# Softmax reciprocals turned on their way through DRAM, unscaled queries, and a later load, in an attention kernel on one core

## Chip, core and metric

The kernel runs on one NeuronCore of a Trainium2 chip; the other seven are idle. The metric is the device time of one launch in microseconds (us). Before the change it is 2303.48 us, the median of three runs (2294.57, 2303.48, 2305.79).

## The reference

One block of a transformer, all in float32, with x of 2048 rows by 256 columns, 16 heads of width 128, and a feed-forward part of width 704. Cut to what is computed:

```python
xn = (x - mean(x)) / sqrt(var(x) + 1e-5)
qkv = xn @ Wqkv.T                          # q, k, v: 2048 x 16 x 128 each
logits = q @ k.T * 128 ** -0.5             # each head: 2048 x 2048
w = softmax(logits)
att = (w @ v) @ Wout.T                     # 2048 x 256
Q(w) = clip(round(w / (mean(|w|) + 1e-8)), -1, 1)
ffn = (sigmoid(xn @ Q(w1).T) * (xn @ Q(w2).T)) @ Q(w3).T
out = x + att + ffn
```

## The kernel before

**Stages.** A lead-in of some 100 us normalizes x, turns it (the tile `xnT`, features on partitions), makes q, k and v of the first heads and does the feed-forward part, whose result waits in DRAM. Then come 64 *blocks*: 16 heads, in each four blocks of 512 queries. A block has four *steps* of 128 queries; `n` numbers blocks, `t` the steps of a block, `h` heads, `b` the block in its head, `v` the steps. Scores run six steps (`LEAD`) ahead of the weighting by v, so one pass of the main loop works on two blocks at once.

**A step of scores** (`scores`): TensorE multiplies the step's 128 queries by all 2048 keys, into two PSUM tiles `s` of 128 x 1024. DVE takes the maximum of each (L630, into the two columns of `mx`) and then the negated larger one (L633, `nm`); ACT takes the exponential with `nm` as bias and the row sums as a second output (L640, into `p`). Sixteen DMAs, ten from SP's queue and six from ACT's (`exchanged`, L659), move the pieces of `p` into `part`, with partitions exchanged, and DVE transposes 32 x 32 blocks of `part` into `R` (L706).

**Weighting.** Products are made by a scheme of the Strassen kind: seven products of half size in place of eight. It needs sums and differences of the operands. POOL makes those of `R` (`differences`, L726: T1, T2, T3 and T4, some in halves), of v once a head (`v_combined`, L748) and of weights and of `xnT` (`weight_sums`, `sums_of`, `x_sums`). TensorE multiplies (`weighted`, L773) into the PSUM tile `av`; ACT copies one half of partial results to SBUF (`copied`, L791, into `oU`) and DVE adds the other (`added`, L799). After the fourth step DVE multiplies by the reciprocals of the row sums (L801), and the block's result is sent to DRAM (`put_away`, L827, tile `od`). It comes back later for the output projection.

**The reciprocals.** `inverses(n)` sums the two halves of the row sums on DVE (L673), takes the reciprocals (L674, four columns of a 32-column tile `ri`), transposes 32 x 32 blocks (L676, into `riT`), and sends four rows from each group of 32 partitions to DRAM with four DMAs from POOL's queue (L678, tile `rd` of 4 x 128). `spread(n)` brings the 512 numbers of a block back to all 128 partitions (L685, into `oT`). The multiply L801 then makes `oT` from `oU` and `oT`.

**Queries and keys of later heads** are made by the same kind of scheme during the steps of the head before. `fast_product` makes one product at a time in a PSUM bank (`ps_m`, one buffer), and `fast_read` adds it on DVE to what stands in `kTs` and `qTs` (L200, L197). Queries carry the factor SCALE = 128 ** -0.5, keys do not; so where a query sum starts from a key sum, `fast_scaled` (L223) copies it with the factor, once for two blocks of a head, 28 times in all.

**Order.** The order on each engine is the order of the code (`manual_schedule`). What a step leaves to do (`left`: `added`, the second read, `fast_scaled`) is done at the head of the next step, ahead of its scores. POOL's order in a block is: at step 0 `put_away` of the block before, T1b, T3b, parts of `v_combined`, and the first half of T2; at step 1 the rest of T2, T4, then `spread`; at step 2 the four DMAs of `inverses` of the next block; at step 3 T1a and T3a of the next block. Between these stand DMAs and sums for other stages (`between`). All of these DMAs are issued by POOL, in order.

**The last head** has no later head's products; its projection is done at once. `fetched_back(b)` brings the feed-forward part and the other heads' sum back (L924, into `xnT`) and x for the final sum (L925, into `sofar`), at step 2 of the block before; `opened(b, ...)` uses both at steps 0 and 3 of the block after (L944: DVE adds to `sofar`). Its last four blocks are multiplied by the reciprocals in `projected` (L964), not at L801.

## Time and profile before

One profiled execution: 2299.23 us by its own time, of which the span from the first to the last instruction is 2297.5 us; the granted TensorE clock was 0.992 of full speed.

| Engine | busy, us | share of the span |
|---|---|---|
| TensorE (PE) | 2189.6 | 95% |
| VectorE (DVE) | 1887.3 | 82% |
| GpSimd (POOL) | 1765.6 | 77% |
| TensorE weight loads (PEld) | 1094.3 | 48% |
| ScalarE (ACT) | 744.9 | 32% |

| Stretch of the span, us | PE busy | DVE busy | POOL busy |
|---|---|---|---|
| 0 to 170 (lead-in, first scores) | 162.07 | 109.90 | 44.28 |
| 170 to 2180 (blocks) | 1920.44 | 1708.12 | 1660.55 |
| 2180 to 2297.5 (last head) | 107.03 | 69.25 | 60.80 |

How to read it: a group is a line of the code, an engine, an operation and `out<-in` by the names of tiles, with the number of instructions, the busy time, the mean duration of one in ns, and the idle time of the engine just before them with what ended it. A wait `X <- Y` says that X's engine stood idle until Y ended. PEld are TensorE's weight loads, which run ahead of the matmuls; PEq, DVEq and so on are the engines' instruction queues; "issue" is time in which nothing that the profile shows was waited for. Matmuls overlap each other, so a busy PE is not PE at its peak. The issue of a DMA by POOL counts as POOL work.

### The profile page before, as it was taken

The numbers are of one execution on the slowest core, as the hardware profiler recorded it, in microseconds if no ns is written. First come the engines' busy times: TensorE is split into PE (matmuls) and PEld (weight loads), VectorE is DVE, ScalarE is ACT, GpSimd is POOL, SyncE is SP. The second block draws the span as 40 slices with busy tenths as digits, with TensorE's granted clock in tenths as the row PEclk, the third lists the DMA queues.
The fourth block names the chain that finished last, engine by engine and source line by source line (L and its number), as shares of the span: only waits on it lengthen the run. The fifth ranks groups of instructions, "written<-read, shape, count | busy, mean of one in ns | idle before, by whom it ended". The sixth has DMA issues, their size and how long they took to land.

```text
span 2297.5 us, 41411 instructions
## 1 busy us (share of the span) xinstructions
PE 2189.6 (95%) x13514; PEld 1094.3 (48%) x13514; DVE 1887.3 (82%) x2562; ACT 744.9 (32%) x1390; POOL 1765.6 (77%) x1376
## 2 busy tenths in 40 slices
PE   9999999999999999899998999999999999999898
PEld 6744444454445444455444544444444544445455
DVE  6577888888788888789888888888888788888764
ACT  5543332333232323323333233332333233323331
POOL 0167878887788887988788887888789788898773
PEclk9999999999999999999999999999999999999999
DMA  2166667676676767776677766767677676776764
GB/s 89 55 151 155 150 179 196 166 208 158 175 205 173 189 161 190 193 193 184 162 184 187 199 175 174 198 173 191 159 183 210 171 185 161 189 194 184 193 172 123
DMA packets 246568, 398.46 MB, mean 173 GB/s; under 512 B 80720, under 2 KB 85264, under 8 KB 246352
## 3 DMA queue, kind: packets, MB, share of 16 engines
q1 hardware_dynamic: 127664, 174.95, 29.9%
q0 software_dynamic: 43792, 118.93, 18.6%
q10 hardware_dynamic: 74896, 101.94, 17.3%
q8 instruction: 106, 1.74, 0.3%
q14 instruction: 110, 0.90, 0.1%
HBM read 77.66 MB, written 49.41 MB: 55 GB/s over the span
## 4 chain that ended last, share of the span: by engine, by line
PE 28%; POOL 23%; DMA 19%; DVE 14%; issue 7%; SPq 5%; ACT 2%; ACTq 2%; DVEq 0%; POOLq 0%
DMA part<-p 17%; POOL R L726 14%; PE s L94 10%; PE av L773 8%; SPq L659 5%; DVE mx L630 4%; DVE R L706 3%; POOL st L748 2%; PE ph L508 2%; ACTq L659 2%; ACT p L640 2%; PE pow L94 1%; DVE oU L799 1%; PE pvw L94 1%; PE pw L94 1%
## 5 line engine op out<-in xcount | busy, mean ns | idle before, releaser
L726 POOL TENSOR_TENSOR R<-R 128x1024 f32<-128x1024 f32 x441 | 1181.6, 2686 | 37.0 <-DVE R L706 17.1
L640 ACT ACTIVATE p<-s,nm 128x1024 f32<-128x1024 f32 x512 | 566.2, 1111 | 1381.8 <-DMA part<-p 924.0
L94 PE MATMUL s<-kT,qT 128*64 128x512 f32 x4000 | 946.2, 594 | 13.9 <-ACT p L640 13.7
L630 DVE TENSOR_REDUCE mx<-s 128x1 f32<-128x1024 f32 x512 | 613.1, 1218 | 182.3 <-PE s L94 168.1
L706 DVE STREAM_TRANSPOSE R<-part 128x1024 f32<-128x1024 f32 x512 | 605.2, 1220 | 48.4 <-DMA part<-p 44.9
L94 PEld LDWEIGHTS s<-kT,qT 128*64 128x64 f32 x4000 | 331.1, 137 | 529.0 <-issue 442.1
L773 PE MATMUL av<-R,st 128*64 128x256 f32 x3024 | 495.9, 388 | 53.7 <-POOL R L726 50.2
L773 PE MATMUL av<-R,v 128*64 128x256 f32 x3728 | 539.7, 379 | 0.4 <-DVE oU L799 0.3
L773 PEld LDWEIGHTS av<-R,v 128*64 128x64 f32 x3728 | 341.9, 137 | 186.5 <-issue 56.7
L773 PEld LDWEIGHTS av<-R,st 128*64 128x64 f32 x3024 | 297.7, 139 | 208.1 <-POOL R L726 77.4
L678 POOL DMA_DIRECT2D rd<-r x240 | 124.8, 527 | 162.4 <-DVE r L676 162.1
L827 POOL DMA_DIRECT2D od<-oT x60 | 34.5, 575 | 157.7 <-DVE oT L801 150.2
L799 DVE TENSOR_TENSOR oU<-av,oU 64x256 f32<-64x256 f32 x248 | 101.1, 408 | 54.5 <-ACT oU L791 51.9
L911 DVE TENSOR_TENSOR osums<-pow,osums 128x512 f32<-128x512 f32 x196 | 124.6, 677 | 0.6 <-PE pow L94 0.6
L791 ACT COPY oU<-av 64x256 f32<-64x256 f32 x248 | 91.0, 367 | 94.4 <-PE av L773 90.1
L94 PE MATMUL pw<-t,ws 128*64 128x512 f32 x336 | 109.2, 592 | 0.0
L640 ACT ACTIVATION_READ_ACCUMULATOR p<-s,nm 128x1 f32 x512 | 100.2, 196 | 0.0
L160 POOL TENSOR_TENSOR t<-xnT 128x512 f32<-128x512 f32 x4 | 5.1, 1270 | 107.2 <-DMA part<-p 107.2
L315 DVE TENSOR_TENSOR v<-pvw,v 128x512 f32<-128x512 f32 x98 | 65.1, 676 | 24.9 <-PE pvw L94 24.9
L94 PE MATMUL pw<-xnT,wk 128*64 128x512 f32 x224 | 67.5, 599 | 14.2 <-DVE kT L200 14.2
L200 DVE TENSOR_TENSOR kT<-pw,kT 128x512 f32<-128x512 f32 x112 | 76.9, 686 | 1.8
L842 POOL TENSOR_TENSOR o<-o 128x512 f32<-128x512 f32 x56 | 71.7, 1280 | 0.5
(165 smaller groups left out, 1630.8 us busy)
## 6 DMA issues: line engine op xcount, KB each, us to landing
part<-p SPq DMA_DIRECT2D x2556, 64.0 KB, 2.2
part<-p ACTq DMA_DIRECT2D x1540, 64.0 KB, 2.5
oT<-rd POOLq DMA_DIRECT2D x60, 256.0 KB, 4.3
od<-oT POOLq DMA_DIRECT2D x60, 256.0 KB, 3.6
o<-od POOLq DMA_DIRECT2D x60, 256.0 KB, 4.4
vd<-v POOLq DMA_DIRECT2D x112, 128.0 KB, 3.6
xnT<-vd POOLq DMA_DIRECT2D x56, 256.0 KB, 5.2
osums<-yd POOLq DMA_DIRECT2D x28, 512.0 KB, 6.2
```

The costliest lines, as they stand in the source:

```text
L94: nc.tensor.matmul(out[c * HP : (c + 1) * HP], lhs[:, c * HP : (c + 1) * HP], rhs, start=start, stop=stop, skip_group_check=True,)
L200: nc.vector.tensor_tensor(k, pk, base, ALU.add)
L630: nc.vector.tensor_reduce(mx[:, i : i + 1], s, AX.X, ALU.max)
L640: nc.scalar.activation(p, s, AF.Exp, bias=nm, accum_out=sums[n][:, t, i : i + 1],)
L659: queue.dma_start(parts[v][g // 2][bass.ts(j, 32), g % 2, :], ps[j // 2][bass.ts(g, 32), bass.ts(j % 2, S // NQ)],)
L678: nc.gpsimd.dma_start(rds[n % 2][:, bass.ts(j, 32)], riT[32 * j : 32 * j + TB, :])
L706: nc.vector.transpose(to[:, t % 2, 2 * i : 2 * i + 2], part.rearrange("p g (s c) -> p g s c", s=2),)
L726: nc.gpsimd.tensor_tensor(o, x, y, ALU.subtract)
L773: nc.tensor.matmul(av[i * HP : (i + 1) * HP, half], l[:, kk], moving(s, kk), start=start, stop=(k == units[r] - 1), skip_group_check=True,)
L791: nc.scalar.copy(u[op, oq], av[ap, half])
L799: nc.vector.tensor_tensor(u[p, q], av[p, half], u[p, q], ALU.add)
L911: nc.vector.tensor_tensor(y, pm, y, ALU.add)
```

## The change

It does four things. (1) `rd` becomes 128 x 32 and `inverses` sends all of `riT` there with one DMA; `spread` reads, for each group of 32 partitions, the first four rows (128 numbers), and puts the four runs side by side in `oT`, so that `oT` now lies in the order (group, step, query in the group); the multiply reads it through a view in turned order. (2) The multiply writes to `oU` in place, and `put_away` sends `oU`; `oT` holds only reciprocals. (3) Queries are kept without SCALE: copies and plain additions stand where scaling ones stood, `fast_scaled` is gone (the first sum of `q1` reads `k1` directly), the exponential has `scale=SCALE`, and `nm` is made by one two-step scalar operation: the larger of the two columns of `mx` times -SCALE. (4) In the last head the load of x is moved from step 2 to step 3.

```diff
@@ q_piece
-        nc.scalar.activation(qT, pm, AF.Copy, scale=SCALE)
+        nc.scalar.copy(qT, pm)
@@ fast_read
         def q_sum(q, base):
-            nc.vector.scalar_tensor_tensor(q, pm, SCALE, base, ALU.mult, ALU.add)
+            nc.vector.tensor_tensor(q, pm, base, ALU.add)
...
         elif (b % 2, i) == (0, 1):
             if not second:
-                q_sum(q1, q0)
+                nc.vector.tensor_tensor(
+                    q1.rearrange("p (k j r) -> p k j r", j=P // 32, r=32), pk, k1, ALU.add
+                )
             else:
                 q_sum(q0, q1)
...
-    def fast_scaled(h: int, b: int):
-        c = b // 2 * 2
-        k1 = kTs[h].rearrange("p (j k r) -> p k j r", j=P // 32, r=32)[:, (c + 1) * TB : (c + 2) * TB]
-        q0 = qTs[h, c].rearrange("p (k j r) -> p k j r", j=P // 32, r=32)
-        nc.vector.tensor_scalar(q0, k1, SCALE, None, ALU.mult)
@@ tiles in DRAM
-    rds = [away.tile([TB, P], F32, tag=f"rd{i}", name=f"rd{i}") for i in range(2)]
+    rds = [away.tile([P, 32], F32, tag=f"rd{i}", name=f"rd{i}") for i in range(2)]
@@ scores
-        nc.vector.tensor_reduce(nm, mx, AX.X, ALU.max, negate=True)
+        nc.vector.tensor_scalar(nm, mx[:, 0:1], mx[:, 1:2], -SCALE, ALU.max, ALU.mult)
...
-                p, s, AF.Exp, bias=nm, accum_out=sums[n][:, t, i : i + 1],
+                p, s, AF.Exp, bias=nm, scale=SCALE, accum_out=sums[n][:, t, i : i + 1],
@@ inverses, spread
         nc.vector.transpose(riT, ri)
-        for j in range(P // 32):
-            nc.gpsimd.dma_start(
-                rds[n % 2][:, bass.ts(j, 32)], riT[32 * j : 32 * j + TB, :]
-            )
+        nc.gpsimd.dma_start(rds[n % 2], riT)
...
-            nc.gpsimd.dma_start(oT, rds[n % 2].rearrange("t p -> (t p)").partition_broadcast(P))
+            r = rds[n % 2].rearrange("(j c) r -> j (c r)", c=32)[:, : TB * 32]
+            nc.gpsimd.dma_start(
+                oT.rearrange("p (j x) -> p j x", j=P // 32), r.partition_broadcast(P)
+            )
@@ added
         if r == 3 and n < NBK - NB:
-            nc.vector.tensor_tensor(oT, u, rbs[n], ALU.mult)
+            u = u.rearrange("p (t j r) -> p t j r", t=TB, r=32)
+            r = rbs[n].rearrange("p (j t r) -> p t j r", t=TB, r=32)
+            nc.vector.tensor_tensor(u, u, r, ALU.mult)
@@ put_away
-        nc.gpsimd.dma_start(ods[h % (2 * G)][b], oT)
+        nc.gpsimd.dma_start(ods[h % (2 * G)][b], oU)
@@ fetched_back, between
         nc.gpsimd.dma_start(xnT[:, :, bass.ts(b, QB)], yds[b])
+
+    def x_fetched(b: int):
         nc.gpsimd.dma_start(
             sofar[b], x[b * QB : (b + 1) * QB, :].rearrange("(t p) d -> p t d", p=P)
         )
...
         if t == 2 and last - 1 <= n < last + NB - 1:
             fetched_back(n + 1 - last)
+        if t == 3 and last - 1 <= n < last + NB - 1:
+            x_fetched(n + 1 - last)
@@ the main loop, in left
-                if seven and product is fast_product and (b % 2, v % TB) == (0, 0):
-                    fast_scaled(h + 1, b)
```

## The prediction

> **What bounds the kernel now.** I read the page first, then the sums of waits, then the chain of waits stretch by stretch. From the page, the engines' busy shares and the chain that ended last:

> ```profile
> PE 2189.6 (95%) x13514; PEld 1094.3 (48%) x13514; DVE 1887.3 (82%) x2562; ACT 744.9 (32%) x1390; POOL 1765.6 (77%) x1376
> PE 28%; POOL 23%; DMA 19%; DVE 14%; issue 7%; SPq 5%; ACT 2%; ACTq 2%; DVEq 0%; POOLq 0%
> ```

> TensorE is busy 95% of 2297.5 us, so 107.9 us of it is idle, lead-in and tail included. What an edit on DVE or POOL can give is that idle time, and only where that engine ends it. The sums of waits say which engine does:

> ```profile
> PEld s L94 <- issue: 442.1, 1563, 0.6
> ...
> PEld av L773 <- POOL R L726: 77.4, 60, 4.6
> ...
> PEld s L94 <- ACT p L640: 40.9, 52, 7.0
> ...
> PEld pw L94 <- DVE kT L200: 27.3, 15, 4.0
> ...
> PEld pw L94 <- DVE qT L197: 13.9, 27, 1.0
> ...
> PEld pvw L94 <- DVE qT L197: 7.7, 14, 0.7
> ```

> (Columns: total us, times, longest.) An ordinary gap between two weight loads is 442.1/1563 = 0.28 us, with no one waited for; only what a wait has beyond it stops TensorE. The change takes work from POOL (L678) and DVE (L223); their costliest rows:

> ```profile
> L678 POOL DMA_DIRECT2D rd<-r x240 | 124.8, 527 | 162.4 <-DVE r L676 162.1
> L223 DVE TENSOR_SCALAR qT<-kT x28: 427/1596/1660, 230.3 to 2065.4; 128x512 f32<-128x512 f32 x28
> ```

> The first (from the page) issues four DMAs a block, 4 x 0.52 = 2.08 us, mostly after POOL has waited about 3 us for L676. The second (the answer on that line; min/median/max ns) is bimodal: 427 ns once, with POOL idle, and 1286 to 1660 ns in the 27 others, each of which began inside a POOL subtraction and ended about 0.3 us after it. At 1045.57 it took 1.60 us while POOL's subtraction begun at 1044.50 still had 1.31 us to run. So L223 waits for POOL.

> **The change, part by part.** The sum is made against the profiled execution: 2299.2 us, span 2297.5 us; that is 4.3 us under the median 2303.5 of the three runs.

> *One transfer of reciprocals (L678).* Three of four issues go. The one that stays covers 128 partitions, like L827 (575 ns mean), so 2.08 - 0.58 = 1.50 us a block, 90 us of POOL in 60 blocks. That counts only where POOL runs without a wait from there until TensorE waits for it. In most blocks the next thing POOL meets is the issue of od, which waits for the multiply (L827 waits 150.2 us in 44 blocks): the saving becomes a longer wait there. It passes where the weight sums and V's combinations fill that wait; the chain shows such a stretch:

> ```profile
> 1075.73 2.05 POOL rd L678 x4
> ...
> 1094.45 1.23 POOL st L748
> 1095.67 4.65 POOL R L726 x2
> 1100.33 0.04 issue
> 1100.37 1.72 PE av L773 x13
> ```

> Between the first and the last of these lines stand only POOL's pieces and short issue times, 25 us of them, and TensorE waits at its end (1.7 us of PE idle in 1094 to 1102). It recurs seven times (near 281, 552, 827, 1098, 1369, 1641, 1914), with 1.7 to 2.2 us of PE idle each: 7 x 1.5 = 10.5 us gained. In the sister stretch near 940 to 968 POOL waits for a landing (xnT<-vd) behind the same issues, so nothing is gained there. The landing of rd matters nowhere: it is read some 26 us later. Bounds: 0 and 77.4, all of the waits for POOL.

> *The spread.* It reads four 512-byte rows where it read 2 KB, so four times the pieces for each partition. Its issue takes 566 ns now; the costliest POOL issue in the trace is L925 at 777 ns, so 0 to 0.2 us a block, 12 us of POOL. It is covered by POOL's 3 us wait for L676 right behind it; without that cover, 7 x 0.2 = 1.4 us. I take 0. The landing (4.3 us) has about 17 us before the multiply.

> *L223 gone.* 28 x 1.463 = 41.0 us off DVE, at the head of a step, ahead of both maxima, nm and the read of the next product (L197), whose bank TensorE needs. Those are the two qT lines above: (13.9 - 27 x 0.28) + (7.7 - 14 x 0.28) = 6.3 + 3.8 = 10 us. What is late next is TensorE itself, whose loads then follow at 0.28 us. Bounds: 0, and 41 if all of L223 were on the path. L197 becomes a plain addition: 684 ns to the 677 to 686 ns of L911 and L200, nothing; the first addition reads k1 where it read q0, the same.

> *nm (L633).* A reduction of two elements, 155 ns, 256 times, becomes a two-step scalar operation with one operand read per partition. One element through such an operation with constants took 153 ns:

> ```profile
> L462 DVE TENSOR_SCALAR neg<-pos x3: 153/153/154, 27.1 to 34.9; 128x1 f32<-128x1 f32 x3
> ```

> An operand per partition adds about 55 ns: an element costs 1.045 ns (L801, 692 ns for 512, against L412, 161 for 4); L475 with such an operand takes 1819 ns for 1536 elements, so 214 beyond its elements, and L411 without one 163 for 4, so 159. That makes 208 ns, +53 ns a step, 14 us of DVE. It meets TensorE where a wait ends on DVE's reads (kT 15, v 8, osums 8 times) or on exponentials that waited for nm (72 of the 242 long waits there, hence some 16 of 52): 47 x 0.053 = 2.5, say 3 us. Bounds: 0 and 14, if it never waits for POOL; that is the rival below. I take the no-wait row because the fixed part of the operations that ran at two elements a cycle is larger: 427 - 267 = 160 ns (L223), and 163 and 162 (L465: 954 ns for 1408 elements, 1020 for 1536, less 55 for the operand). L462 has 153 - 1 = 152: it looks like the ordinary mode, and DVE's one-input work in that mode did not wait for POOL: L676 takes 211 to 213 ns in all 60 blocks.

> [...] No row of this trace shows a one-element operation beside POOL.

> *Result kept in oU, sent from oU.* The multiply keeps its size (L801: 693 ns median, up to 1693 where POOL runs beside it). But ACT's first copy of the next block (L791) now waits until od has been read. Matching rows: od is issued 0.99 us after the multiply starts, lands 3.6 us later (2.7 to 6.0), and the copy starts at about 6.3 us: 1.8 us to spare at the median. In 11 of 60 blocks the landing would be late, 8.1 us together, 2.0 at most. Behind the copy on ACT stand six exchange DMAs and the next exponentials; TensorE needs it only after the next 3.4 us of scores. I take 2 us; bounds 0 and 8.1.

> *x a step later.* Three of the four loads now queue on POOL behind T1a and T3a. From 2160.2, 2196.0, 2235.0 and 2268.4 they move to about 2170, 2204.9, 2240.6 and 2268.4. With landings of 8.5 us (5.6 to 12.2), and the additions (L944) at 2180.2, 2212.5, 2245.3 and 2279.0, DVE waits about 0, 0.9, 3.8 and 0 us; the transposes behind it wait 1.6 and 1.9 us for the exchange anyway. 2 us; bounds 0 and 9.

> *Scale in the exponential.* An immediate in the same ACT instruction; the eight activations that made q (604 ns) become copies (587). Zero.

> Sum: -10.5 - 10 + 3 + 2 + 2 = -13.5: 2299.2 - 13.5 = **2286 us**, 0.6% down.

> **The rivals.** (1) *nm waits for POOL as L223 does: slower.* In 165 of the 256 steps a POOL addition or subtraction was running when L633 began, with 200 us left in all; less the 0.14 us that L223's start-up hides, 177 us of waits. L223's 41 us showed 10 us on TensorE, a quarter; but a wait in every step, on the way to the exponential, has less slack behind it, so between a quarter and a half: +44 to +89. From -16.5 (the sum without nm) that is 2327 to 2372, say 2342 at a third. Deciding point: above about 17 us of the 177 on the path, the gain is gone. For: L223's rows. Against: L462's fixed part. (2) *The waits close up elsewhere: no change.* Both gains are ends of waits where something else may stand just behind, as the multiply does for most of the 90 us. Half the gains and the costs as above: -10 + 7 = -3, 2296. (3) *More than the gaps counted*: all of the qT gaps (21.6) and two further POOL stretches near 1505 and 1778, 3 us: -21.6 - 13.5 + 7 = -28, 2271.

> **How the numbers follow.** Forecast 0.50, its own range 2276 to 2296; (1) 0.25; (2) 0.15; (3) 0.10. Below 2270 and above 2335 I leave some 2 in 10, the upper part of (1). 0.5%, about what a measurement of this kernel can tell from no change, is 11.5 us. Faster by more: 0.36 of the forecast's half, and (3): 0.46. Within: 0.13 of it, and 0.11 of (2): 0.24. Slower: (1), and the rest: 0.30.

> **What would show it.** Right: no L223; L678 once a block; nm near 208 ns with no second mode; the waits of "pw" and "pvw" for qT nearly gone; av's waits for POOL down by about 10 us; POOL's waits for L676 and L801 longer. Wrong: nm at 0.5 to 2.5 us wherever POOL subtracts, DVE's busy time above 1887 us, exponentials waiting for nm far beyond 371 us.

## The result and the profile after

The changed kernel takes 2310.03 us (median of 14 runs, 2305.85 to 2316.43) against 2296.15 us (14 runs, 2290.73 to 2305.79): ratio 1.0059, 95% interval 1.0046 to 1.0071. It is slower by some 13.5 us (0.0059 x 2296), where 13.5 us less were forecast. The profiled execution took 2305.85 us, its span is 2304.1 us, and the granted clock was 0.989 of full speed (0.992 before).

From the profile's page, the engines' busy shares and the chain that ended last:

```profile
PE 2187.8 (95%) x13514; PEld 1165.5 (51%) x13514; DVE 1867.2 (81%) x2534; ACT 744.1 (32%) x1390; POOL 1678.5 (73%) x1196
PE 38%; POOL 22%; DMA 20%; DVE 7%; issue 5%; SPq 4%; ACT 2%; ACTq 1%; DVEq 0%; POOLq 0%
```

POOL has lost 87.1 us of work and DVE 20.1, as the prediction wanted, and yet TensorE is idle for 116.3 us in place of 107.9. The sums of TensorE's waits (total us, times, longest):

```profile
PEld av L769 <- POOL R L722: 62.1, 56, 4.1
PEld pw L94 <- DVE kT L200: 51.9, 15, 5.7
...
PEld s L94 <- ACT p L636: 37.8, 43, 4.9
...
PEld pvw L94 <- DVE qT L197: 5.8, 14, 1.1
```

The wait for POOL has shrunk by 15.3 us, the pw line for qT is gone. One line has grown much: the products `pw` wait for kT, 51.9 us where it was 27.3. (The shrinking is not the forecast gain: the same line is 74.0 us in one_issue_2k below, which also has the single issue, and 61.5 and 55.5 us in two_spreads_2k and one_issue_1k, which are slower still. It shrinks in the kernels whose TensorE is held up at kT.) DVE and POOL themselves now wait for transfers (DVE's line with xnT was 10.3 us before, POOL's 2.0, the one for wo 0.7):

```profile
POOL vd L318 <- DMA xnT<-vd: 25.5, 15, 3.3
DVE v L327 <- DMA xnT<-vd: 23.8, 22, 3.5
POOL wos L268 <- DMA wo<-in_woutT_dram: 16.9, 7, 2.9
```

The edits themselves did what they say. One issue of `rd` a block (page, costliest groups), and `nm` with its durations (min/median/max ns; the answer on that line):

```profile
L673 POOL DMA_DIRECT2D rd<-r x60 | 33.4, 557 | 148.6 <-DVE r L672 148.6
L629 DVE TENSOR_SCALAR nm<-mx x256: 212/214/217, 104.5 to 2262.6; 128x1 f32<-128x1 f32 x128
```

What has changed for the worse is the spread. Its landing is 5.8 us after the issue where it was 4.3 (the page's list of DMA issues; the last number is the median). Before the change:

```profile
oT<-rd POOLq DMA_DIRECT2D x60, 256.0 KB, 4.3
...
xnT<-vd POOLq DMA_DIRECT2D x56, 256.0 KB, 5.2
```

and after it:

```profile
oT<-rd POOLq DMA_DIRECT2D x60, 256.0 KB, 5.8
...
xnT<-vd POOLq DMA_DIRECT2D x56, 256.0 KB, 5.7
```

The second row hides two kinds. The 28 loads of `xnT` that are issued within 3.5 us behind a spread (two behind each of 14 spreads) went from a median of 5.68 to 7.22 us; the other 28 from 4.57 to 4.20.

One place shows how that reaches TensorE. POOL's timeline (start, us, what; idle time before it and what ended it in brackets):

```profile
936.33 0.77 POOL L679 DMA_DIRECT2D oT<-rd  x1
937.10 0.71 POOL L83 DMA_DIRECT2D wo<-in_woutT_dram  x1
...
939.04 1.11 POOL L322 DMA_DIRECT2D xnT<-vd  x2
...
944.49 0.45 POOL L268 TENSOR_TENSOR wos<-wo 128x128 f32<-128x128 f32 x1 [2.68 <-DMA wo<-in_woutT_dram]
```

and DVE's and TensorE's of the same time:

```profile
946.62 0.71 DVE L327 STREAM_TRANSPOSE v<-xnT 128x512 f32<-128x512 f32 x1 [3.65 <-DMA o<-od]
948.40 0.71 DVE L327 STREAM_TRANSPOSE v<-xnT 128x512 f32<-128x512 f32 x1 [1.07 <-DMA xnT<-vd]
...
949.88 0.69 DVE L200 TENSOR_TENSOR kT<-pw,kT 128x512 f32<-128x512 f32 x1
```

```profile
950.63 1.97 PE L94 MATMUL pw<-xnT,wk 128*64 128x512 f32 x4 [4.82 <-DVE kT L200]
```

The spread goes out at 936.33, the loads of `wo` and `xnT` behind it. DVE stands 3.65 and then 1.07 us before its transposes of v, which read `xnT`. They start 0.12 and 0.02 us after its two loads have landed, 7.46 and 8.77 us after their issue; the load of `o` that the profile names for the first wait landed later than the transpose began. The read of kT (L200) is queued behind these transposes, and TensorE needs the bank that it empties: 4.82 us of idle time. At the same place before the change (TensorE then waits 1.78 us):

```profile
941.38 0.71 DVE L331 STREAM_TRANSPOSE v<-xnT 128x512 f32<-128x512 f32 x1 [1.59 <-DMA rd<-r]
943.55 0.71 DVE L331 STREAM_TRANSPOSE v<-xnT 128x512 f32<-128x512 f32 x1 [1.46 <-DMA xnT<-vd]
```

All of DVE's waits before these transposes come to 36.7 us, 15.1 before the change, and each ends within 0.25 us behind a landing of `xnT`. TensorE's waits for kT on the matmuls come 16 times, 40.8 us together (13 and 14.2 before). This kT wait is the line that has grown.

A second cost hangs on the first. The stretches around this stall (us, then the busy time of PE, PEld, DVE, ACT and POOL; behind POOL's stand the granted clock, the DMA share and GB/s):

```profile
942.67:946.09 3.42, 3.14 (x15) 1.23 (x11) 0.30 (x1) 0.00 (x0) 1.52 (x4) 1.00 1.06 254
946.09:949.50 3.41, 0.00 (x0) 0.00 (x0) 1.80 (x4) 0.00 (x0) 1.90 (x5) 1.00 0.88 206
949.50:956.33 6.83, 5.70 (x22) 2.66 (x24) 6.40 (x8) 2.56 (x5) 6.66 (x5) 0.50 0.63 169
```

After this window of 3.41 us without a matmul the clock was granted at half for 6.83 us. From the page's clocks, (1 - 0.989) x 2304.1 = 25 us of the span are lost to half clock after the change, (1 - 0.992) x 2297.5 = 18 us before.

### The profile page after: what moved, and what is told of

Its sections match the earlier page's. It is cut to its first block, busy times and chain, and to the rows that moved or that the text cites. A ratio compares the mean times of both kernels' runs of the same rounds, so it can differ in the third digit from the quotient of the medians.

```text
span 2304.1 us, 41234 instructions
## 1 busy us (share of the span) xinstructions
PE 2187.8 (95%) x13514; PEld 1165.5 (51%) x13514; DVE 1867.2 (81%) x2534; ACT 744.1 (32%) x1390; POOL 1678.5 (73%) x1196
## 4 chain that ended last, share of the span: by engine, by line
PE 38%; POOL 22%; DMA 20%; DVE 7%; issue 5%; SPq 4%; ACT 2%; ACTq 1%; DVEq 0%; POOLq 0%
DMA part<-p 15%; POOL R L722 14%; PE s L94 13%; PE av L769 12%; SPq L655 4%; PE pw L94 3%; DVE R L702 3%; DMA xnT<-vd 3%; POOL st L744 2%; PE ph L504 2%; PE pvw L94 2%; ACTq L655 1%; POOL vd L318 1%; ACT p L636 1%; DMA vd<-v 1%
## 5 line engine op out<-in xcount | busy, mean ns | idle before, releaser
L94 PE MATMUL s<-kT,qT 128*64 128x512 f32 x4000 | 952.5, 594 | 15.4 <-ACT p L636 15.2
L94 PEld LDWEIGHTS s<-kT,qT 128*64 128x64 f32 x4000 | 370.3, 137 | 490.7 <-issue 378.3
L769 PE MATMUL av<-R,v 128*64 128x256 f32 x3728 | 550.5, 384 | 0.8 <-DVE oU L795 0.6
L769 PE MATMUL av<-R,st 128*64 128x256 f32 x3024 | 486.6, 383 | 41.4 <-POOL R L722 38.3
L769 PEld LDWEIGHTS av<-R,v 128*64 128x64 f32 x3728 | 351.0, 139 | 186.9 <-issue 62.0
L825 POOL DMA_DIRECT2D od<-oU x60 | 33.4, 557 | 161.9 <-DVE oU L799 161.9
L673 POOL DMA_DIRECT2D rd<-r x60 | 33.4, 557 | 148.6 <-DVE r L672 148.6
L94 PE MATMUL pw<-t,ws 128*64 128x512 f32 x336 | 108.9, 592 | 2.1 <-DVE kT L200 2.1
L94 PE MATMUL pw<-xnT,wk 128*64 128x512 f32 x224 | 73.6, 653 | 38.7 <-DVE kT L200 38.7
L318 POOL DMA_DIRECT2D vd<-v x112 | 61.9, 558 | 28.7 <-DMA xnT<-vd 25.5
L200 DVE TENSOR_TENSOR kT<-pw,kT 128x512 f32<-128x512 f32 x112 | 76.9, 686 | 1.8
```

Of the source, the lines that this page charges most:

```text
L94: nc.tensor.matmul(out[c * HP : (c + 1) * HP], lhs[:, c * HP : (c + 1) * HP], rhs, start=start, stop=stop, skip_group_check=True,)
L200: nc.vector.tensor_tensor(k, pk, base, ALU.add)
L318: nc.gpsimd.dma_start(vd[q], v[bass.ts(q, 32)].rearrange("r (j c) -> r j c", c=S // 8))
L769: nc.tensor.matmul(av[i * HP : (i + 1) * HP, half], l[:, kk], moving(s, kk), start=start, stop=(k == units[r] - 1), skip_group_check=True,)
```

## The experiments

Theory Q: the spread in 512-byte runs takes longer on the DMA engines, and what is queued behind it on POOL's queue lands later. Rivals: W, the write over 128 partitions; N, `nm`; U, sending `oU`, with ACT's copy behind it; I, the spread's longer issue on POOL; D, short runs hold up transfers wherever the spread stands; X, the later load of x. Each kernel was run 4 to 12 times. A ratio is to the kernel before, run beside it, whose median moved between 2295 and 2299 us; kernels are compared by their ratios, and 0.01 is 23 us.

**one_issue_2k.** After, with the order turned on the way out: one write puts the numbers in (step, query) order, and the spread reads 2 KB runs as before.

```diff
-    rds = [away.tile([P, 32], ...)]
+    rds = [away.tile([32, P], ...)]
-        nc.gpsimd.dma_start(rds[n % 2], riT)
+        nc.gpsimd.dma_start(rds[n % 2].rearrange("c (j r) -> j c r", r=32), riT)
-            r = rds[n % 2].rearrange("(j c) r -> j (c r)", c=32)[:, : TB * 32]
-            nc.gpsimd.dma_start(oT.rearrange("p (j x) -> p j x", j=P // 32), r.partition_broadcast(P))
+            r = rds[n % 2][:TB].rearrange("t p -> (t p)")
+            nc.gpsimd.dma_start(oT, r.partition_broadcast(P))
-            nc.vector.tensor_tensor(u, u, r, ALU.mult)       # turned views
+            nc.vector.tensor_tensor(u, u, rbs[n], ALU.mult)
```

> The changed kernel, but with the reciprocals written to DRAM in the order (step, query), still by one transfer of 128 rows, so that the spread reads one run of 2 KB for each partition again and the multiply reads oT in plain order. Theory Q (the spread in four runs of 512 B holds POOL's DMA queue longer, and what is queued behind it lands about 1.5 us later: V's pieces, weights, the running sum): the spread lands after 4.3 us in place of 5.8, xnT<-vd behind it after about 5.7 us in place of 7.2, DVE's waits at V's transposes go from 36.6 us back to about 15, and the time falls by 20 to 28 us from the changed kernel, to 2283 to 2291, below the kernel before by 5 to 13. Rival W (the write of 128 rows of 128 bytes, landing after 4.1 us in place of 2.7, delays the queue): the time stays within 4 us of the changed kernel, 14 above before. Rival N (53 ns more for nm in every step): the same, 14 above before. Rival U (ACT waits until od has been read out of oU): the same, 14 above before.

Measured: 2280.43 us (2278.14 to 2282.67), ratio 0.9938 [0.9923, 0.9953], 14 us faster than before. `nm`, `oU`, the scale and the later x are all in it, so the loss lies in the form of the spread: 1.0059 - 0.9938 = 0.0121, 28 us. Two other things differ between the two kernels, and neither weighs: the multiply through turned views takes 693 ns at the median, as the plain one does in before and here, and POOL is as busy (1675.7 us, 1678.5 in after), because the turned write takes 736 ns to issue where the plain one takes 557. The spread lands after 4.3 us, the `xnT` behind it after 5.75. The waits of TensorE and DVE are about those of before (27.3 and 10.3 us); POOL's for `xnT` (2.0 us before) stays longer:

```profile
PEld pw L94 <- DVE kT L200: 29.3, 15, 3.9
...
POOL vd L318 <- DMA xnT<-vd: 12.2, 14, 1.5
DVE v L327 <- DMA xnT<-vd: 10.5, 13, 2.7
```

The span is 23.8 us shorter than after's: TensorE's idle time 10.2 (116.3 to 106.1), its busy time 13.6 (2187.8 to 2174.2, the same 13514 matmuls). Of the latter about 9 are clock: (1 - 0.993) x 2280.3 = 16 us lost, against 25.

**four_issues_512.** The other side: before, with its four writes, and the spread in 512-byte runs.

```diff
-                rds[n % 2][:, bass.ts(j, 32)], riT[32 * j : 32 * j + TB, :]
+                rds[n % 2][32 * j : 32 * j + TB, :], riT[32 * j : 32 * j + TB, :]
-            nc.gpsimd.dma_start(oT, rds[n % 2].rearrange("t p -> (t p)").partition_broadcast(P))
+            r = rds[n % 2].rearrange("(j c) r -> j (c r)", c=32)[:, : TB * 32]
+            nc.gpsimd.dma_start(oT.rearrange("p (j x) -> p j x", j=P // 32), r.partition_broadcast(P))
```

with `rd` of 128 x 32 as in after, and the multiply through turned views into `oU`, which is sent.

> The kernel before with four issues for the reciprocals as it had, but each into its own rows of a tile of 128 x 32, so that the spread reads four runs of 512 B as in the changed kernel; the multiply reads oT through the turned view and writes to oU, which is sent. No scale edit, no later load of x. Theory Q: 15 to 28 us above the kernel before (2311 to 2324), since the spread's cost comes without the gains; spread landing 5.8 us, xnT<-vd behind it 7.2 us. Rival W: as the kernel result_in_oU, since the write is the old one. Rival N: as result_in_oU. Rival U: 14 above before, as result_in_oU.

Measured: 2316.04 us (2315.41 to 2321.13), ratio 1.0102 [1.0082, 1.0121]. The spread alone costs 1.0% on the old kernel, with no scale edit, no `nm` and no single write in it; W, N and X are out as its cause. The same line grows:

```profile
PEld pw L94 <- DVE kT L200: 51.0, 15, 5.1
```

**result_in_oU** and **scale_in_exp** do one part each: before with the multiply into `oU` and `oU` sent; before with all of the scale edit (no L223, new `nm`).

```diff
-            nc.vector.tensor_tensor(oT, u, rbs[n], ALU.mult)
+            nc.vector.tensor_tensor(u, u, rbs[n], ALU.mult)
-        nc.gpsimd.dma_start(ods[h % (2 * G)][b], oT)
+        nc.gpsimd.dma_start(ods[h % (2 * G)][b], oU)
```

> The kernel before with the multiply writing to oU in place and oU sent, alone. Theory Q, rivals W and N: 0 to 4 us above before. Rival U: 10 to 15 above before, with ACT's copies waiting for od in many blocks.

> The kernel before with the scale edit alone: unscaled queries, no L223, nm by a scalar operation, scale in the exponential. Theory Q and the prediction's terms: -10 for L223 and +3 for nm, so 7 below the kernel before (2284 to 2292), waits of pw and pvw for qT down from 21.6 us. Rival N: 10 to 15 above before. Rivals W and U: 7 below before.

Measured: 2294.52 us, 0.9995 [0.9981, 1.0010], and 2291.93 us, 0.9977 [0.9962, 0.9992]. U costs nothing that can be told apart, though ACT's copy does wait for `od` (11.7 us in 9 blocks). The scale edit is worth 0.2%, some 5 us; the qT line of pw is gone, that of pvw is 5.1 us (7.7 before).

**spread_behind.** After, with the spread still in 512-byte runs but issued last in its step.

```diff
-            spread(n)              # ahead of the step's other transfers
...
+        if t == 1:
+            spread(n)              # behind them
```

> The changed kernel with the spread issued as the last transfer of its step: the weights, V's pieces and the running sum that are issued in the same step now go ahead of it; the spread keeps its four runs of 512 B and its issue time. Theory Q (those behind it in POOL's queue land late): xnT<-vd of that step lands after 4.2 to 5 us in place of 7.2, and the time falls by 20 to 30 us from the changed kernel, to 2280 to 2290. Rival I (the spread's issue, 776 ns in place of 566 on POOL, 60 times): the issue stays, so the time stays within 5 us of the changed kernel, 2305 to 2315. Rival D (the small pieces cost all transfers time wherever they stand): within 8 us of the changed kernel.

Measured: 2287.10 us (2283.23 to 2290.81), ratio 0.9962 [0.9948, 0.9976]: 1.0% is won back (1.0059 - 0.9962, 22 us) though the spread lands after 6.07 us, later than in after. The loads of `xnT` now stand ahead of it and land in 4.52 us:

```profile
PEld pw L94 <- DVE kT L200: 14.2, 14, 1.6
```

So it is not the spread's own reader that pays.

**one_issue_2k_pad** puts two 128x64 memsets on POOL behind each spread of one_issue_2k (POOL's busy time +19 us, more than the 13 us of the longer issue).

```diff
+            for _ in range(2):
+                nc.gpsimd.memset(pad, 0.0)
```

> The kernel one_issue_2k with two small memsets on POOL (128 x 64) behind each spread, some 0.2 to 0.3 us of POOL in each of 60 blocks, in place of the issue time that the 512-byte spread cost. Theory Q and rival D: within 4 us of one_issue_2k, 2277 to 2285. Rival I: 15 to 25 us above it, 2295 to 2305.

Measured: 2278.01 us, 0.9926 [0.9908, 0.9944], no slower than one_issue_2k. Rival I is out.

**one_issue_2k_x_early** loads x at step 2 again.

```diff
-        if t == 3 and last - 1 <= n < last + NB - 1:
             x_fetched(n + 1 - last)      # now in the branch of step 2
```

> The kernel one_issue_2k with x loaded at step 2 as before. The prediction's term: the later load costs 2 us, so this is 0 to 4 us below one_issue_2k (2276 to 2281). Rival X (the later load lets the running sum xnT<-yd land earlier, a gain): 1 to 5 us above it. Theory Q says nothing of it beyond rival X.

Measured: 2279.81 us, 0.9932 [0.9911, 0.9952]: the later load makes no difference that can be told. X is out.

**one_issue_2k_behind.** one_issue_2k with the spread issued last in its step (the edit of spread_behind).

> The kernel one_issue_2k with its 2 KB spread issued as the last transfer of its step. Theory Q: the 2 KB spread holds the queue too, some 1.2 us for those behind it (5.7 us in place of 4.5), so the time falls a little more, by 3 to 12 us, to 2268 to 2278. Rivals I and D: no change, within 3 us of one_issue_2k.

Measured: 2268.99 us (2266.02 to 2272.28), ratio 0.9879 [0.9855, 0.9903], the fastest kernel of this study. So 2 KB runs ahead of the loads cost too, 0.6% here. And the 18 us between this and spread_behind speak for D: with the same place in the queue short runs still cost. Neither Q nor D alone covers both results: with short runs the place is worth 22 us, and behind the others the run length is worth 18. How the 18 us reach TensorE is not shown; no single wait of the matmuls grows by more than 6 us. The exchange DMAs of SP and ACT that are issued in the 2.5 us behind a spread land after 5.8 and 5.9 us (means) in spread_behind and 4.5 and 4.9 us here; away from spreads they take 2.8 and 2.9. DVE's waits for them are 43.1 against 32.3 us.

**two_spreads_2k.** one_issue_2k with the spread sent twice in 2 KB runs, the second time to a spare tile that nobody reads: large runs, but twice the work ahead of the loads.

```diff
             nc.gpsimd.dma_start(oT, r.partition_broadcast(P))
+            nc.gpsimd.dma_start(xds[n % 2], r.partition_broadcast(P))
```

> one_issue_2k with the spread sent twice, the second time in the same 2 KB runs to a spare tile in DRAM that nobody reads: the same number of bytes in large runs, twice over, right behind the first. Theory (engine time ahead in the queue delays what is queued behind): the second transfer takes the place of the slower pieces, the xnT<-vd behind lands about 1.2 to 2 us later than 5.75 us, exchanges on the other queues too, pw's waits for kT rise to 45 to 55 and 30 to 40 us, and the time to 2298 to 2312 us, near after's 2310, though the spread that the multiply reads lands as early as in one_issue_2k. If it is the small runs as such, or the spread's own landing at the multiply: 2280 to 2283 us.

Measured: 2318.96 us (2312.37 to 2326.98), ratio 1.0087 [1.0071, 1.0102]. The spread that is read lands after 4.2 us, and still the kernel loses 1.5% (1.0087 - 0.9938), 34 us, against one_issue_2k, more than expected. The loads of `xnT` within 3.5 us behind the first spread (21 here) take 6.66 us, and the known line is back:

```profile
PEld pw L94 <- DVE kT L200: 58.9, 15, 5.7
```

The second issue also takes POOL 34 us (1709.5 against 1675.7), but TensorE's wait for POOL's `R` does not grow, it falls from 74.0 to 61.5 us. Here more time on the DMA engines ahead of the loads was enough (the packets of POOL's transfers, q0 on the page, take 22.2% of the 16 engines' span, 18.8% in one_issue_2k); short runs are another way to make it.

**one_issue_1k.** one_issue_2k with the numbers in two halves: two writes (`rd` is 64 x 64), the spread in two runs of 1 KB for a partition, a turned multiply.

```diff
+        for g in range(2):
+            nc.gpsimd.dma_start(rds[n % 2][bass.ts(g, 32)].rearrange("c (j r) -> j c r", r=32), riT[bass.ts(g, P // 2), :])
...
+            r = rds[n % 2].rearrange("(h c) x -> h (c x)", h=2)[:, : TB * 64]
+            nc.gpsimd.dma_start(oT.rearrange("p (h x) -> p h x", h=2), r.partition_broadcast(P))
```

> one_issue_2k with the reciprocals in two halves (query groups 0 and 1, 2 and 3): two writes in place of one, the spread in two runs of 1 KB to a partition, the multiply through a turned view. Dose and response of the run length. Theory (the spread's time on the DMA engines goes with the number of runs): its landing and that of the xnT<-vd behind it about a third of the way from 2 KB to 512 bytes, so 4.8 and 6.2 us, and the time a third of the way from 2280 to 2310, 2288 to 2293 us. If there is a threshold between 512 bytes and 1 KB: like one_issue_2k, landing 4.3 us, 2280 to 2283 us (a second write issue of 0.56 us a block makes up to 3 us). If any turned view or any split costs the whole: 2305 to 2310 us.

Measured: 2328.24 us (2321.14 to 2331.19), ratio 1.0123 [1.0107, 1.0139], slower than all three expectations. The dose was wrong: a spread's 64 packets of 4 KB take 278 ns each in before and 275 in one_issue_2k (2 KB runs), 567 in 1 KB runs, 534 in 512-byte runs (medians over the 60 spreads). So 1 KB runs cost as much as 512-byte ones: the landing is 5.73 us, the `xnT` behind it 7.42. That makes it like after; the 15 us beyond that (1.0123 - 1.0059) are not separated. In the profile the two writes cost POOL 1.40 us a block (0.56 in after), and 35 us are lost to half clock (25 in after).

**before_one_issue** and **before_spread_behind** do the two good parts alone on the old kernel: one write with a 2 KB spread; the old spread issued last in its step.

```diff
-        for j in range(P // 32):
-            nc.gpsimd.dma_start(rds[n % 2][:, bass.ts(j, 32)], riT[32 * j : 32 * j + TB, :])
+        nc.gpsimd.dma_start(rds[n % 2].rearrange("c (j r) -> j c r", r=32), riT)
```

> Before, with the reciprocals written by one transfer in the order (step, query) and the spread left as it is, in runs of 2 KB; nothing else of the change. The prediction's first term (seven stretches of 1.5 us): 2296 - 10.5 = 2285.5 us. By the difference of the runs so far (one_issue_2k 2280.4 against 2296 less the 3 to 5 us of the scale edit): -9 to -12, so 2284 to 2287. If the saving on POOL closes up elsewhere: 2296, and the 15 us of one_issue_2k would have to come from the other edits together. In the trace POOL's busy time should fall by some 70 to 80 us, and av's waits for POOL R by about 5 us or less.

> Before, with its own 2 KB spread and its four writes, the spread issued last in its step, behind the step's other transfers; nothing else. The theory that a spread delays what is queued behind it says that before pays a part of this too: the load of xnT<-vd behind it should land at 4.4 to 4.6 us in place of 5.7, pw's waits for kT fall from 27 and 14 us to about 14 and 3, and the time by 8 to 12 us (as one_issue_2k against one_issue_2k_behind), to 2284 to 2288 us. If only 512-byte runs delay others: 2296, no change.

Measured: 2286.53 us (2285.12 to 2289.74), 0.9947 [0.9935, 0.9959], as expected; and 2299.83 us (2295.49 to 2304.77), 1.0001 [0.9991, 1.0010], which was not. In the second the wait that was to fall did fall, and the time did not:

```profile
PEld av L773 <- POOL R L726: 81.8, 57, 4.9
...
PEld pw L94 <- DVE kT L200: 13.1, 14, 1.8
```

Compared block by block (from one block's multiply to the next), 7 us are won in all in the seventh blocks of each group of eight, and 9 and 6 us lost in the eighth and the first, where TensorE waits for POOL at the end of a long run of POOL's work. The largest loss is near 1236: 4.46 us of waiting ahead of the matmuls at 1236.54, where before has 1.41 us ahead of those at 1234.47 (and 1.0 us more than here in each of the two waits beside it). TensorE came to this wait 1.0 us earlier and POOL 2.1 us later: POOL had stood 0.73 us ahead of its transfers `vd`, a wait that the profile puts down to the late spread. On one_issue_2k, whose POOL has 1.4 us a block less to issue (0.74 in place of 2.1), the same edit gives some 13 us. That the room on POOL makes this difference is argued, not shown.

## Why the prediction was wrong

**The step that failed** is the spread: "so 0 to 0.2 us a block, 12 us of POOL. ... I take 0. The landing (4.3 us) has about 17 us before the multiply." What it says of these two holds. The issue grew by 0.21 us (566 to 776 ns mean), and padding of more than that costs nothing; the landing grew by 1.5 us, which the sentence did not foresee, but the multiply never waited for it (it starts some 15 us behind the issue at the median, not 17). But the spread was judged by its own issue and its own reader alone, and nobody asked what is queued behind it. In 14 of the 60 blocks it has two loads of `xnT` behind it on POOL's queue, in seven of these `wo` too, and the exchanges beside it on the DMA engines, and the V transposes, the read of kT and TensorE at the end of that. The term measures +28 us (after against one_issue_2k) and about +25 us on the old kernel (four_issues_512 against result_in_oU: 1.0102 - 0.9995), about 4 us for each of seven pairs of heads. The notice was in the trace: the loads of `xnT` behind a spread already took 5.68 us and the others 4.57.

**The rest of the sum held in size.** Without the spread's loss it is the -13.5 us forecast, and one_issue_2k, which has all else of the change, measured 0.9938, -14 us. Part of this agreement is luck: the single parts measured -12 and -5, some 17 together, and the largest did not come by its forecast path.
- One transfer, -10.5: 0.9947, -12 us on the old kernel. But the line named for it, av's wait for POOL, did not move there (77.4 to 77.5 us), and at the seven places named TensorE's idle time before these matmuls fell from 13.1 to 11.1 us only, where 10.5 us less were forecast. The gain showed as 5 us less idle time and, from (1 - 0.994) x 2284.5 = 14 against 18 us, some 4 us less half clock. The size was right, its path was not the one forecast and stays open.
- L223 gone and `nm`, -10 + 3 = -7: measured -5 (0.9977; the interval allows 2 to 9). `nm` takes 214 ns where 208 was worked out.
- `oU` sent, +2, and x a step later, +2: neither can be told from 0.

**Rival 1** (`nm` waits for POOL) is refuted by the trace. All 256 instructions took 212 to 217 ns, the 197 beside a POOL addition or subtraction as well as the others, and DVE's busy time fell. The wait that L223 showed before (1286 to 1660 ns in 27 of 28 instructions, 427 in the one with POOL idle) did not show in this one-element operation. (Of the prediction's other figures, two elements a cycle are 0.52 ns an element, from L465's 1020 - 954 ns for 128 elements, half of the 1.045 from L801; and L676, which it has at 211 to 213 ns in all 60 blocks, took up to 216; that changes nothing.) So the time came out slower, but not for the reason that carried the chance of slower; that this chance came true is luck. **Rival 2** (waits close up elsewhere, so half the gains) did not happen to the sum of this change, but did to before_spread_behind.

**What no step had** is the clock. In the profiles a window of 3.41 us in which TensorE stood idle for some 2 us or more (limits below) was followed by 3.41 or 6.83 us of half clock, so such a stall was paid a second time. Of the profile's 23.8 us between after and one_issue_2k, some 9 are half clock; the mean clock of all 14 runs of after is 0.989, that of one_issue_2k's 6 runs 0.9945, which is 13 of the 28 us (0.0055 x 2300).

## What to carry to other kernels

A transfer whose layout changes is costed by what is queued behind it on its queue and beside it on the DMA engines, as well as by its own reader: list the transfers of the next 3 to 4 us and who waits for each. Turn an order on the small side (16 KB written once) and leave the large side (256 KB broadcast) in long runs (0.9938 against 1.0059 here); and issue a transfer whose reader comes 15 us later behind those that are awaited at once. What that gives depends on what stands next in line (0 us on the old kernel, some 13 us on one_issue_2k). Where stalls of TensorE come near the 2 us in a window of 3.41 us that half clock followed here, look at the granted clock too: of the 23.8 us between after and one_issue_2k some 9 were half clock.
